# A perceiver-style kernel on one Trainium2 core: the context keys of the first cross attention transposed in 32x32 blocks on VectorE and put in place by copies

## The chip, the core and the metric

The kernel runs on one core of one Trainium2 chip, as one program. The metric is the device time of that program in microseconds. Shown are the median of three runs and, apart from it, one profiled execution, from which all durations come. The engines are called by the names of the profile: PE (TensorE's matmuls) and PEld (its weight loads), DVE (VectorE), ACT (ScalarE), POOL (GpSimd) and SP (SyncE, which here only issues DMAs).

## What is computed

A sequence `x` of 32 batches of 64 tokens with 256 features passes six layers, each added to `x`: a cross attention to a context of 256 tokens per batch, a linear attention, a gated feed-forward layer, a second cross attention, a recurrent layer and a mixture of experts. All is float32. The change touches the first layer alone, and the loading of the second layer's weights. The first layer, cut to what matters:

```python
x_ = layer_norm(context, ln1_g, ln1_b)      # 32 x 256 x 256
l  = layer_norm(layernorm(x), ln2_g, ln2_b) # 32 x 64 x 256
q  = l @ Wq                                 # 16 heads of 64
k, v = split(concat([x_, l], axis=1) @ Wkv) # 320 keys
w  = softmax((q * 64**-0.25) @ (k * 64**-0.25).T)
out = (w @ v) @ Wo
x  = x + out
```

## The kernel before

**Stages.** The first stage (until about 850 us) is this cross attention, batch by batch. Then linear attention, feed-forward, second cross attention and recurrence run together, interleaved over groups of two token tiles, and at the end the experts.

**The first stage.** Keys and values are never formed. A head's query is multiplied with the key weights instead, which gives a 256-wide vector `qk` per query and head, and scores are `qk` against the normalised context itself. The steps, by function:

- `l0_context(t)` loads the context of two batches into `cx` (two buffers), normalises it in place (`norm`) and applies the affine part on POOL (`affine`, two operations on 128 x 1024).
- `l0_queries(g)` does the same for four batches of latents, transposes them on PE (`tr_lat`), forms `q` (PE groups `pq`, evicted by ACT or DVE with the factor 0.125) and then `qk`: eight groups `pqk` per four batches, one per pair of heads, two PSUM banks each, so sixteen evictions.
- `l0_keys(b, ...)` makes `cT`, the transposed context of a batch (2 x 128 features by 256 tokens) followed by the 64 transposed latents. The context's four 128x128 blocks are transposed on PE (`tr_c`, against the identity) and one copy brings the bank to `cT` (two buffers). The latents come by one POOL copy.
- `l0_scores(b, ...)` runs eight PE groups `sc`, 128 rows (two heads x 64 queries) by 320 keys. For each, DVE takes the negated maximum (`nmax`), ACT the exponential with its sum. For every four groups DVE takes the reciprocal of the sums, scales (128 x 1280) and transposes in 32x32 blocks into `bT`, which has one buffer. Then sixteen block copies of 32 x 640 bring `bT` into `pT`: four on POOL, four on ACT or DVE, eight as DMAs issued by SP.
- `l0_applied(b, ...)` multiplies the context with `pT` (PE groups `pu`, four banks per batch) into `uT`; `l0_projected(t, ...)` applies value and output weights (`po`, `pw`) and adds to `x`.

**What sets the order.** The Python code does not issue instructions as it runs. Every operation is recorded in a plan (`Plan`), with a `rank` (its due time in units of a batch), and `run` then issues all of them in one order: at each step the operation that can start first by the planner's own cost table, the lower rank at a tie. An operation made with `either` or `copy` may go to ACT or DVE, whichever starts it first. The hardware executes each engine's instructions strictly in the order issued, each waiting for its own semaphores. Hence all instructions in the profile bear the line of the one place that issues them (L375), and groups are told apart by tile names.

**Memory.** Tiles of the large stages lie at fixed places of one `arena` of 45056 floats per partition. `ar.put(phase, tag, size, *at)` declares the places of a tag. Areas of a later phase may overlap those of an earlier one; their tiles then wait until every tile of the earlier tag has been released. PSUM has eight banks, shared by all.

Of the kernel before, what the change touches and what calls it, by code (L numbers as in the profile page):

```python
# [8 lines left out]
F32 = mybir.dt.float32  # L9
I32 = mybir.dt.int32  # L10
AF = mybir.ActivationFunctionType
ALU = mybir.AluOpType
AX = mybir.AxisListType

P = 128
B, S, D = 32, 64, 256
S2 = 256
# [192 lines left out]
class Plan:  # L210
# [12 lines left out]
    def __init__(self, tc):  # L223
        self.tc, self.ops, self.slots, self.news = tc, [], {}, []
        self.rank, self.group, self.lane, self.last = 0.0, None, None, {}
        for engine, attr in self.ENGINES.items():
            setattr(self, attr, PlanEngine(self, engine))
# [71 lines left out]
    def run(self, ahead):  # L299
# [7 lines left out]
        while todo:  # L307
            best, short = None, None
            while rest[-1] not in waiting:
                rest.pop()  # L310
            for op in sorted(ready, key=lambda op: op.rank):
                if short is not None and op.rank > short.rank and "PE" in op.ways and op.news:
                    continue
                if op.rank > rest[-1].rank + ahead:
                    continue
                at = 0.0
                if op.news and not self.has_room(op):
                    if "PE" in op.ways and (short is None or op.rank < short.rank) and self.has_room(op, True):
                        short = op
                    continue  # L320
                for engine, (length, _) in op.ways.items():
                    at = free[engine]
                    for other in op.before:
                        at = max(at, other.end if other.on == engine and other.end == other.done else other.done + self.HOP)
                    for t_ in op.uses:
                        at = max(at, t_.free_at)
                    key = at, op.rank
                    if best is None or key < best[0]:
                        best = key, op, engine
            assert best is not None, "nothing can start"  # L330
            (at, _), op, engine = best
            length, calls = op.ways[engine]
            todo -= 1
            ready.remove(op)
            waiting.remove(op)
            op.on = engine
            op.end = op.done = free[engine] = at + length
            busy[engine] += length
            if "dma" in calls[0][0]:
                size = PlanEngine.size_of(calls[0])  # L340
                wire = max(wire, op.end) + size / 380e3
                op.done = max(wire, op.end + size / 220e3) + (2.4 if engine == "POOL" else 1.5)
            self.issue(op, engine, calls)
            for other in op.after:
                other.left -= 1
                if other.left == 0:
                    ready.append(other)
# [91 lines left out]
class PlanEngine:  # L439
# [34 lines left out]
    def length(engine, name, args, kw):  # L474
# [18 lines left out]
        if engine == "POOL":  # L493
            return 0.7 if n < 64 else 0.3 + 2.0e-3 * n
        return 0.18 if name == "transpose" else max(0.36, 1.67e-3 * n)
# [3 lines left out]
def kernel(ctx: ExitStack, tc: tile.TileContext, d: dict, out: bass.AP):  # L499
# [130 lines left out]
    with ExitStack() as sa:  # L630
# [15 lines left out]
        for n in range(4):  # L646
            ar.put(1, f"W{n}", 2048, 2048 * n)
        ar.put(1, "q", 2048, 8192)
        ar.put(1, "gb", 1024, 10240)
# [12 lines left out]
        for tag, size, *at in (  # L662
            ("f_wg", 1536, 0), ("s_w", 512, 1536), ("f_wu", 1536, 2048), ("s_wp", 256, 3584), ("m_wr", 16, 3840),
            ("x_wq", 512, 4096), ("x_wk", 512, 4608), ("x_wv", 512, 5120), ("x_wo", 512, 5632), ("f_wd", 1536, 6144),
# [13 lines left out]
            ("g_tmp", 128, 41472), ("g_tmp2", 128, 41600), ("g_h", 128, 41728),  # L678
            ("a_wq", 512, 42496), ("a_wkv", 1024, 43008), ("rows_a", 1024, 44032),
        ):  # L680
# [38 lines left out]
        for t in range(2):  # L719
            pl.sync.dma_start(out=x[t], in_=d["x"][t * P : (t + 1) * P, :])  # L720

        wk = ar.tile([P, KD, 1024], F32, tag="q", name="wk")
        load_w(wk, "l0x_wkv", slice(0, 1024))
# [50 lines left out]
        def l0_context(t):  # L774
# [12 lines left out]
            if t == 2:  # L787

                nxt["a_wq"] = ar.tile([P, KD, D], F32, tag="a_wq", name="a_wq")
                pl.sync.dma_start(out=nxt["a_wq"], in_=d["a_wq"].rearrange("(k p) n -> p k n", p=P))  # L790
# [11 lines left out]
        def l0_queries(g):  # L802
# [20 lines left out]

            q = ar.tile([P, 8, G * S], F32, tag="q", name=f"q{g}")
            for j2 in range(4):
                pl.rank = G * g - 3.0 + 0.5 * j2
                pq = bank([P, 2, G * S], f"pq{g}_{j2}")
                with pl.together(1.75):
                    for jj in range(2):
                        for kd in range(KD):  # L830
                            mm(
                                pq[:, jj],
                                wq[:, kd, (2 * j2 + jj) * P : (2 * j2 + jj + 1) * P],
                                lt[:, kd, :],
                                start=(kd == 0),
                                stop=(kd == KD - 1),
                            )
                o = q[:, 2 * j2 : 2 * j2 + 2, :]
                pl.either(("mul", (o, pq, 0.125), {}), ("tensor_scalar", (o, pq, 0.125, None, ALU.mult), {}))
            pl.rank = G * g - 0.9  # L840
            qk = [None] * 8
            for n in range(8):
                j = 2 * (n % 4) + n // 4
                qk[j] = ar.tile([P, KD, G, 2, S], F32, tag="qk", name=f"qk{g}_{j}")
                pqk = [bank([P, KD, G * S], f"pqk{g}_{j}_{i}") for i in range(2)]
                with pl.together(1.0):
                    for kd in range(KD):
                        for i in range(2):
                            h_ = slice(64 * i, 64 * i + 64)
                            mm(pqk[i][:, kd], wkT[h_, j, kd * P : (kd + 1) * P], q[h_, j, :], start=True, stop=True)  # L850
                for i in range(2):
                    pl.copy(qk[j][:, :, :, i, :], pqk[i].rearrange("p k (b s) -> p k b s", b=G))
            return la, ls, lt, qk

        def l0_keys(b, lt, cx):

            pl.rank, pl.lane = b - 1.2, "k"
            b2, b4 = b % 2, b % G
            cT = ar.tile([P, KD, SK], F32, tag="cT", name=f"cT{b}")
            pst = bank([P, KD, S2], f"tr_c{b}")  # L860
            with pl.together(T4):
                for kd in range(KD):
                    for i in range(2):
                        tr(pst[:, kd, i * P : (i + 1) * P], cx[:, 2 * b2 + i, kd * P : (kd + 1) * P], ident)
            pl.gpsimd.tensor_copy(cT[:, :, S2:SK], lt[:, :, b4 * S : (b4 + 1) * S])
            pl.copy(cT[:, :, 0:S2], pst)
            return cT

        def l0_scores(b, cT, qk):
# [6 lines left out]
            pl.lane = "s"  # L876
            B_ = 32
            bT = ar.tile([P, 5, 4, 4, B_], F32, tag="bT", name=f"bT{b}")
            for jj in range(2):
                pr = ar.tile([P, 4, SK], F32, tag="pr", name=f"pr{b}_{jj}")  # L880
                sm = sp.tile([P, 4], F32, tag="sm", name=f"sm{b}_{jj}")
                for jp in range(4):
                    j = 2 * jp + jj
                    pl.rank = b - 1.6 + 0.1 * (4 * jj + jp)
                    sc = bank([P, SK], f"sc{b}_{j}")
                    with pl.together(1.1):
                        for kd in range(KD):
                            mm(
                                sc,
                                qk[j][:, kd, b % G].rearrange("p i s -> p (i s)"),  # L890
                                cT[:, kd, :],
                                start=(kd == 0),
# [8 lines left out]
                for n in range(2):  # L901
                    pl.vector.transpose(
                        bT[:, 2 * n + jj].rearrange("p k j c -> p j k c"),
                        pr[:, :, n * P : (n + 1) * P].rearrange("p j (k c) -> p j k c", c=B_),
                    )
# [5 lines left out]
            for n in range(4):  # L911
                for a in range(4):
# [4 lines left out]
                    )  # L917
                    if n == 0:
                        pl.gpsimd.tensor_copy(o, i_)
                    elif n < 2:  # L920
                        pl.copy(o, i_)
                    else:
                        pl.sync.dma_start(out=o, in_=i_)
            return pT
# [26 lines left out]
        def l0_projected(t, uT):  # L951
            pl.rank, pl.lane = 2 * t + 1.6, "p"
            oT = ar.tile([P, 8, P], F32, tag="oT", name=f"oT{t}", bufs=1)
            for j4 in range(2):
                po = bank([P, 4, P], f"po{t}_{j4}")
                with pl.together(1.87):
                    for jj in range(4):

                        j = 4 * j4 + jj
                        at = 4 * (j % 2) + j // 2  # L960
                        for kd in range(KD):
                            for i in range(2):
                                mm(
                                    po[64 * i : 64 * i + 64, jj, :],
                                    wv[:, kd, j * P + 64 * i : j * P + 64 * i + 64],
                                    uT[:, kd, at, i].rearrange("p b s -> p (b s)"),
                                    start=(kd == 0),
# [966 lines left out]
```

## Time and profile before

| | |
|---|---|
| median of three runs | 1628.32 us (1628.05 to 1630.23) |
| profiled execution, time | 1633.02 us |
| profiled execution, span from first to last instruction | 1631.3 us |
| mean granted TensorE clock | 0.991 |
| busy: PE, PEld, DVE, ACT, POOL | 97%, 68%, 67%, 43%, 26% |
| moved by DMA | 95.02 MB, mean 58 GB/s |

The page of the profile also divides the span into 40 slices; each digit is the busy share in tenths (9 is 90% or more), `PEclk` the granted clock:

```
PE   8999999999999999999989999999999999999996
PEld 6556656565665656666556777777776777878885
DVE  6657666676766757776755788888888788762230
ACT  4434344353533535334421454454544547432332
POOL 5123123230333223331311221221212112223342
PEclk9999999999999999999999999999999999999998
```

The first stage is slices 1 to 21. Busy time of PE is modelled, since matmuls are pipelined. In the profile a float32 matmul appears as two records (`sc`: 512 matmuls, 1024 records), a transpose as one (`tr_c`: 128). Groups of instructions are written `out<-in`, with the shape as partitions x elements, the count, the busy time and the mean of one, and after a bar the engine's idle time just before them with what ended it. In the timeline the columns are start, duration, engine, and the merged instructions; in square brackets stands how long the engine had been idle and who released it.

### The profile page before, as it was taken

To read this page: it belongs to the slowest core of one execution; us is meant where nothing else is said; L and a number is where in the kernel's file an instruction comes from. 1 tells how busy PE (TensorE), PEld (TensorE's weight loads), DVE (VectorE), ACT (ScalarE), POOL (GpSimd) and SP (SyncE) were. 2 spreads that over 40 slices of the span, in tenths; PEclk is the share of its full clock that TensorE was granted. 3 is DMA by queue.
4 is the path that set the end of the run, shared out by engine and by line. 5 is a ranking of instruction groups with operands and counts; after the bars stand their busy time and mean duration, and the time that the engine had idled before them with its cause. 6 is when DMAs were issued, how large, how long until landed. Compare 5 with 4: busy or idle time off the path is not lost. (4 is left out here: it accounts for less than half of the span.)

```text
span 1631.3 us, 25951 instructions
## 1 busy us (share of the span) xinstructions
PE 1579.4 (97%) x9226; PEld 1106.8 (68%) x9226; DVE 1088.2 (67%) x3089; ACT 693.8 (43%) x1813; POOL 422.1 (26%) x524
## 2 busy tenths in 40 slices
PE   8999999999999999999989999999999999999996
PEld 6556656565665656666556777777777776878885
DVE  6657666676766757776755788888888788762230
ACT  4434344353533535334421454454544547432332
POOL 5123123230333223331311221221212112223342
PEclk9999999999999999999999999999999999999998
DMA  6112112121112211122121000010000220455391
GB/s 212 38 30 59 38 31 44 38 59 29 39 30 46 47 34 40 30 71 53 38 54 49 14 27 27 18 37 14 27 27 20 85 80 19 133 144 141 69 307 31
DMA packets 95601, 95.02 MB, mean 58 GB/s; under 512 B 9327, under 2 KB 85936, under 8 KB 95472
## 3 DMA queue, kind: packets, MB, share of 16 engines
q1 hardware_dynamic: 89952, 85.41, 19.2%
q0 software_dynamic: 5520, 7.94, 2.4%
q8 instruction: 74, 1.21, 0.3%
q14 instruction: 55, 0.45, 0.1%
HBM read 63.63 MB, written 7.47 MB: 44 GB/s over the span
## 5 line engine op out<-in xcount | busy, mean ns | idle before, releaser
L375 PE MATMUL pu<-arena 128*128 128x512 f32 (+1 forms) x768 | 301.0, 615 | 3.5 <-ACT arena L375 2.8
L375 PE MATMUL sc<-arena 128*128 128x320 f32 x1024 | 290.5, 436 | 0.0
L375 PEld LDWEIGHTS sc<-arena 128*128 128x128 f32 x1024 | 190.8, 190 | 95.3 <-issue 19.2
L375 ACT ACTIVATE arena<-sc,nmax 128x320 f32<-128x320 f32 x256 | 134.4, 527 | 250.3 <-DVE nmax L375 241.8
L375 PEld LDWEIGHTS pu<-arena 128*128 128x128 f32 (+1 forms) x768 | 113.9, 189 | 175.9 <-issue 159.1
L375 POOL COPY arena<-arena 32x640 f32<-32x640 f32 (+1 forms) x161 | 108.9, 676 | 404.1 <-DVE arena L375 300.4
L375 DVE TENSOR_REDUCE nmax<-sc 128x1 f32<-128x320 f32 x256 | 121.8, 484 | 105.5 <-PE sc L375 104.1
L375 POOL TENSOR_TENSOR arena<-arena 128x1024 f32<-128x1024 f32 (+3 forms) x72 | 118.5, 1646 | 166.6 <-DVE arena L375 109.7
L375 ACT ACTIVATE arena<-arena,xnm 128x256 f32<-128x256 f32 x256 | 127.1, 500 | 52.1 <-DVE xnm L375 51.9
L375 DVE COPY arena<-pu 128x512 f32<-128x512 f32 x62 | 42.7, 689 | 115.4 <-PE pu L375 115.2
L375 DVE CUSTOM_DVE_ANT_0 arena<-xsc,arena 128x256 f32<-128x256 f32 x256 | 101.2, 421 | 17.7 <-ACT arena L375 10.3
L375 DVE TENSOR_TENSOR arena<-arena,sm 128x1280 f32<-128x1280 f32 x64 | 108.1, 1690 | 2.2
L375 DVE STREAM_TRANSPOSE arena<-arena 128x512 f32<-128x512 f32 (+1 forms) x192 | 104.4, 594 | 3.6
L375 ACT COPY arena<-pu 128x512 f32<-128x512 f32 x66 | 38.4, 585 | 128.0 <-PE pu L375 128.0
L375 POOL DMA_INDIRECT out<-arena x25 | 39.6, 1585 | 102.8 <-DVE arena L375 71.2
L375 PE MATMUL pqk<-arena 64*128 64x256 f32 x512 | 63.1, 383 | 1.6 <-ACT arena L375 1.6
L375 PE MATMUL xpTp<-ident,arena 128*128 128x128 f32 x512 | 63.6, 274 | 0.9 <-ACT arena L375 0.9
L375 PE MATMUL xak<-arena 128*128 128x512 f32 x128 | 62.3, 610 | 0.0
L375 PEld LDWEIGHTS xpTp<-ident,arena 128*128 128x128 f32 x512 | 56.9, 141 | 7.2 <-DVE arena L375 2.2
L375 PE MATMUL xav<-arena 128*128 128x256 f32 x256 | 61.5, 384 | 0.0
L375 PEld LDWEIGHTS po<-arena 128*64 128x64 f32 x1024 | 55.5, 137 | 8.8 <-issue 8.3
L375 PE MATMUL mepha<-arena 128*128 128x256 f32 x256 | 60.1, 385 | 1.4 <-ACT arena L375 1.4
(395 smaller groups left out, 2800.9 us busy)
## 6 DMA issues: line engine op xcount, KB each, us to landing
arena<-in_m_w SPq DMA_DIRECT2D x26, 1024.0 KB
arena<-arena SPq DMA_DIRECT2D x256, 80.0 KB
arena<-in_ctx SPq DMA_DIRECT2D x32, 256.0 KB
arena<-in_ctxT SPq DMA_DIRECT2D x16, 512.0 KB
x<-in_x SPq DMA_DIRECT2D x16, 128.0 KB
arena<-in_l0x_wkv SPq DMA_DIRECT2D x2, 1024.0 KB
arena<-arena SPq DMA_DIRECT2D x16, 128.0 KB
out<-x SPq DMA_DIRECT2D x16, 128.0 KB
```

The costliest lines, as they stand in the source:

```text
L375: r = getattr(real, name)(*[get(a) for a in args], **{k: get(a) for k, a in kw.items()})
```

## The change

Four things are changed.

1. **Keys.** For every batch but the first, `l0_keys` no longer uses PE. DVE transposes the context in 32x32 blocks into a new tile `bC` (two buffers): two instructions of 128 x 512. Sixteen copies of 32 x 128 then bring the blocks to their partitions in `cT`: four on POOL, twelve on ACT or DVE (`move` with `min(n, 1)`, so never as DMAs). The rank of the keys goes from `b - 1.2` to `b - 2.6`. `cT` has a new layout, `[P, 5, KD, S]`, in which a score's 320 keys stand in another order; the transposes of the probabilities undo it. The POOL copy of the latents becomes contiguous.
2. **Queries.** `q` is four tiles with a buffer each instead of one; `wk`, which had shared `q`'s place, gets one of its own in phase 0. Heads are taken in plain order 0 to 7 in `qk`, scores and projection, instead of even pairs before odd ones.
3. **Late loads.** The loads of `a_wq`, `a_wkv`, `rows_a` and `rows` (some 1.7 MB), recorded with the third pair of batches, get rank 29.5 and move in SP's queue from the start to between batches 20 and 28. `a_wq` and `a_wkv` take over the place that `q` had; `xTa` and `qT` of the second stage move to the place of `bC`, `q` and one free place.
4. **Planner.** Its cost for a POOL copy goes from `0.3 + 2.0e-3 n` to `0.2 + 0.9e-3 n` us. A field `lean` is added to the choice between ACT and DVE; it stays 0.

The core of the diff:

```diff
-            return 0.7 if n < 64 else 0.3 + 2.0e-3 * n
+            return 0.7 if n < 64 else 0.2 + 0.9e-3 * n if name == "tensor_copy" else 0.3 + 2.0e-3 * n
...
-        ar.put(1, "q", 2048, 8192)
+        ar.put(0, "wk", 2048, 25856)
+        ar.put(1, "q", 512, 8192, 8704, 9216, 9728)
+        ar.put(1, "bC", 512, 42496, 43008)
...
-            ("xTa", 512, 8192, 8704), ("qT", 512, 9216, 9728), ("xn0a", 256, 10240), ("xn1a", 256, 10496),
+            ("xTa", 512, 42496, 43008), ("qT", 512, 9728, 43520), ("xn0a", 256, 10240), ("xn1a", 256, 10496),
...
-            ("a_wq", 512, 42496), ("a_wkv", 1024, 43008), ("rows_a", 1024, 44032),
+            ("a_wq", 512, 8192), ("a_wkv", 1024, 8704), ("rows_a", 1024, 44032),
...
             if t == 2:
 
+                pl.rank = 29.5
                 nxt["a_wq"] = ar.tile([P, KD, D], F32, tag="a_wq", name="a_wq")
...
+        def move(n, o, i):
+            if n == 0:
+                pl.gpsimd.tensor_copy(o, i)
+            elif n == 1:
+                pl.copy(o, i)
+            else:
+                pl.sync.dma_start(out=o, in_=i)
...
         def l0_keys(b, lt, cx):
             pl.rank, pl.lane = b - 1.2, "k"
             b2, b4 = b % 2, b % G
-            cT = ar.tile([P, KD, SK], F32, tag="cT", name=f"cT{b}")
-            pst = bank([P, KD, S2], f"tr_c{b}")
-            with pl.together(T4):
+            pl.rank = b - 2.6
+            cT = ar.tile([P, 5, KD, S], F32, tag="cT", name=f"cT{b}")
+            pl.gpsimd.tensor_copy(cT[:, 4], lt[:, :, b4 * S : (b4 + 1) * S])
+            if b == 0:
...
+                return cT
+            bC = ar.tile([P, 4, KD, 2, B_], F32, tag="bC", name=f"bC{b}")
+            for i in range(2):
+                pl.vector.transpose(
+                    bC[:, :, :, i].rearrange("p k d c -> p d k c"),
+                    cx[:, 2 * b2 + i].rearrange("p (d k c) -> p d k c", d=KD, c=B_),
+                )
+            for n in range(4):
+                for a in range(4):
+                    k = (a + n) % 4
+                    move(
+                        min(n, 1),
+                        cT[B_ * k : B_ * k + B_, a].rearrange("p d c -> p (d c)"),
+                        bC[B_ * a : B_ * a + B_, k].rearrange("p d i c -> p (d i c)"),
+                    )
             return cT
...
-                    j = 2 * jp + jj
+                    j = 4 * jj + jp
...
-                        pr[:, :, n * P : (n + 1) * P].rearrange("p j (k c) -> p j k c", c=B_),
+                        pr[:, :, 0:S2].rearrange("p j (k i c) -> p i j k c", i=2, c=B_)[:, n],
```

As built, the changed kernel has 4 `tr_c` matmuls instead of 128, 62 more DVE transposes, and 496 copies of 32 x 128: 160 on DVE, 212 on ACT, 124 on POOL. From the first group of the second stage's keys and values (`lakv`) on, PE's instructions stand in the old order.

More of the change, by code (lines that the diff above doesn't have):

```diff
@@ L224, in __init__ @@
         self.tc, self.ops, self.slots, self.news = tc, [], {}, []
-        self.rank, self.group, self.lane, self.last = 0.0, None, None, {}
+        self.rank, self.group, self.lane, self.last, self.lean = 0.0, None, None, {}, 0.0
         for engine, attr in self.ENGINES.items():
@@ L326, in run @@
                         at = max(at, t_.free_at)
-                    key = at, op.rank
+                    key = at + (self.lean if engine == "DVE" and len(op.ways) > 1 else 0.0), op.rank
                     if best is None or key < best[0]:
@@ L720 @@
             pl.sync.dma_start(out=x[t], in_=d["x"][t * P : (t + 1) * P, :])
-        wk = ar.tile([P, KD, 1024], F32, tag="q", name="wk")
+        wk = ar.tile([P, KD, 1024], F32, tag="wk", name="wk")
         load_w(wk, "l0x_wkv", slice(0, 1024))
@@ L822, in l0_queries @@
             pl.copy(lt, pst)
[L824 to L829, printed above, removed]
-                        for kd in range(KD):
[L831 to L852, printed above, removed]
@@ L853, in l0_queries @@
-            return la, ls, lt, qk
+            q, qk = [None] * 4, [None] * 8
+            for step in range(5):
+                if step < 4:
+                    pl.rank = G * g - 3.0 + 0.5 * step
+                    q[step] = ar.tile([P, 2, G * S], F32, tag="q", name=f"q{g}_{step}")
+                    pq = bank([P, 2, G * S], f"pq{g}_{step}")
+                    with pl.together(1.75):
+                        for jj in range(2):
+                            for kd in range(KD):
+                                mm(
+                                    pq[:, jj],
+                                    wq[:, kd, (2 * step + jj) * P : (2 * step + jj + 1) * P],
+                                    lt[:, kd, :],
+                                    start=(kd == 0),
+                                    stop=(kd == KD - 1),
+                                )
+                    o = q[step]
+                    pl.either(("mul", (o, pq, 0.125), {}), ("tensor_scalar", (o, pq, 0.125, None, ALU.mult), {}))
+                pl.rank = G * g - 0.9
+                for j in range(8) if step == 4 else ():
+                    qk[j] = ar.tile([P, KD, G, 2, S], F32, tag="qk", name=f"qk{g}_{j}")
+                    pqk = [bank([P, KD, G * S], f"pqk{g}_{j}_{i}") for i in range(2)]
+                    with pl.together(1.0):
+                        for kd in range(KD):
+                            for i in range(2):
+                                h_ = slice(64 * i, 64 * i + 64)
+                                mm(
+                                    pqk[i][:, kd],
+                                    wkT[h_, j, kd * P : (kd + 1) * P],
+                                    q[j // 2][h_, j % 2, :],
+                                    start=True,
+                                    stop=True,
+                                )
+                    for i in range(2):
+                        pl.copy(qk[j][:, :, :, i, :], pqk[i].rearrange("p k (b s) -> p k b s", b=G))
@@ L855, in l0_keys @@
+            return la, ls, lt, qk
+        B_ = 32
+        def move(n, o, i):
[5 more added lines that the diff above has]
+                pl.sync.dma_start(out=o, in_=i)
         def l0_keys(b, lt, cx):
@@ L858, in l0_keys @@
             b2, b4 = b % 2, b % G
-            cT = ar.tile([P, KD, SK], F32, tag="cT", name=f"cT{b}")
-            pst = bank([P, KD, S2], f"tr_c{b}")
-            with pl.together(T4):
-                for kd in range(KD):
[L863 to L866, printed above, removed]
+            pl.rank = b - 2.6
+            cT = ar.tile([P, 5, KD, S], F32, tag="cT", name=f"cT{b}")
+            pl.gpsimd.tensor_copy(cT[:, 4], lt[:, :, b4 * S : (b4 + 1) * S])
+            if b == 0:
+                pl.rank = b - 1.2
+                pst = bank([P, KD, S2], f"tr_c{b}")
+                with pl.together(T4):
+                    for kd in range(KD):
+                        for i in range(2):
+                            tr(pst[:, kd, i * P : (i + 1) * P], cx[:, 2 * b2 + i, kd * P : (kd + 1) * P], ident)
+                for kd in range(KD):
+                    pl.copy(
+                        cT[:, 0:4, kd, :].rearrange("p a (i c) -> p a i c", i=2),
+                        pst[:, kd, :].rearrange("p (i a c) -> p a i c", i=2, a=4),
+                    )
+                return cT
+            bC = ar.tile([P, 4, KD, 2, B_], F32, tag="bC", name=f"bC{b}")
+            for i in range(2):
+                pl.vector.transpose(
+                    bC[:, :, :, i].rearrange("p k d c -> p d k c"),
+                    cx[:, 2 * b2 + i].rearrange("p (d k c) -> p d k c", d=KD, c=B_),
+                )
+            for n in range(4):
[5 more added lines that the diff above has]
+                        bC[B_ * a : B_ * a + B_, k].rearrange("p d i c -> p (d i c)"),
+                    )
             return cT
@@ L876, in l0_scores @@
             pl.lane = "s"
-            B_ = 32
             bT = ar.tile([P, 5, 4, 4, B_], F32, tag="bT", name=f"bT{b}")
@@ L890, in l0_scores @@
                                 qk[j][:, kd, b % G].rearrange("p i s -> p (i s)"),
-                                cT[:, kd, :],
+                                cT[:, :, kd, :],
                                 start=(kd == 0),
@@ L917, in l0_scores @@
                     )
[L918 to L923, printed above, removed]
+                    move(n, o, i_)
             return pT
@@ L959, in l0_projected @@
                         j = 4 * j4 + jj
-                        at = 4 * (j % 2) + j // 2
                         for kd in range(KD):
@@ L965, in l0_projected @@
                                     wv[:, kd, j * P + 64 * i : j * P + 64 * i + 64],
-                                    uT[:, kd, at, i].rearrange("p b s -> p (b s)"),
+                                    uT[:, kd, j, i].rearrange("p b s -> p (b s)"),
                                     start=(kd == 0),
```

## The prediction, made before the changed kernel was run

> **What bounds the kernel now.** I read the page's busy rows first, then a table of windows, then TensorE's waits, then the transposes' own rows, and last the timeline at the two places where TensorE waits at all. The windows (busy time of PE, PEld, DVE, ACT, POOL, with counts, then granted clock and DMA) cover the start, two steady stretches of four batches each, and the end of the first stage:
>
> ```profile
> 0.00:100.00 100.00, 88.76 (x405) 59.11 (x406) 66.11 (x154) 43.51 (x103) 37.25 (x54) 0.98 0.39 114
> 420.00:524.00 104.00, 103.77 (x501) 65.50 (x500) 70.55 (x138) 44.23 (x107) 29.10 (x30) 1.00 0.19 39
> 524.00:628.00 104.00, 103.77 (x502) 65.54 (x501) 70.84 (x138) 44.23 (x107) 29.32 (x30) 1.00 0.18 39
> 800.00:900.00 100.00, 94.13 (x465) 59.20 (x464) 59.05 (x153) 23.41 (x56) 16.68 (x33) 0.97 0.21 50
> ```
>
> TensorE works 103.77 of 104 us; VectorE 68%, ScalarE 43%, GpSimd 28%. A busy PE row alone proves little, so here are TensorE's waits between 100 and 780 us (total, times, longest):
>
> ```profile
> PE pqk L375 <- ACT arena L375: 1.6, 7, 0.2
> PE pu L375 <- DVE arena L375: 0.6, 3, 0.2
> ```
>
> 2.2 us in 680: the stage runs at the pace of TensorE's queue, and work taken from that queue is worth its own time, as long as no other engine then ends a wait last. These two rows name where that would happen: the evictions of `pqk` by ScalarE, and `pu`, which needs the transposed probabilities `pT`.
>
> **Removed: 31 of 32 context transposes.** Four `tr_c` matmuls per batch; only batch 0 keeps them. In the timeline at 429 us, first a `pqk` place:
>
> ```profile
> 429.15 0.60 PE L375 MATMUL tr_c<-ident,arena 128*128 128x128 f32 x4
> 429.36 0.49 DVE L375 TENSOR_REDUCE nmax<-sc 128x1 f32<-128x320 f32 x1 [0.58 <-PE sc L375]
> 429.68 6.74 PE L375 MATMUL pqk<-arena 64*128 64x256 f32 x58
> ...
> 431.46 0.17 DVE L375 RECIPROCAL sm<-sm 128x4 f32<-128x4 f32 x1
> 431.66 1.49 DVE L375 TENSOR_TENSOR arena<-arena,sm 128x1280 f32<-128x1280 f32 x1
> 431.71 2.54 ACT L375 COPY arena<-pqk 128x512 f32<-128x512 f32 x5 [0.23 <-PE pqk L375]
> ...
> 434.52 1.47 ACT L375 COPY arena<-arena 32x640 f32<-32x640 f32 x2 [0.27 <-DVE arena L375]
> ...
> 436.02 2.06 ACT L375 COPY arena<-pqk 128x512 f32<-128x512 f32 x4
> ...
> 436.66 1.13 PE L375 MATMUL pqk<-arena 64*128 64x256 f32 x6 [0.23 <-ACT arena L375]
> ```
>
> The four start at 429.15 and the next work at 429.68: 0.53 us of TensorE's queue. At 485.33 two contexts stand together and `pq` follows at 486.21: 0.44 each. I take 0.49: 31 x 0.49 = **15.2 us**. [...]
>
> **Added.** Per batch: two VectorE transposes of 512 elements, 4 GpSimd copies and 12 copies on ScalarE or VectorE, all 32x128. The rows of 100 to 780 us that are nearest:
>
> ```profile
> L375 ACT COPY arena<-arena 32x640 f32<-32x640 f32 x52 | 37.6, 722 | 11.2 <-DVE arena L375 10.0
> L375 DVE COPY arena<-arena 32x640 f32<-32x640 f32 x52 | 43.4, 834 | 1.2
> L375 DVE STREAM_TRANSPOSE arena<-arena 128x512 f32<-128x512 f32 x104 | 67.9, 690 | 2.9
> L375 POOL COPY arena<-arena 128x128 f32<-128x128 f32 x26 | 8.8, 338 | 71.5 <-PE sc L375 71.1
> ```
>
> No 32x128 copy is in the trace on ACT or DVE. Bounds: not under 128/640 of the row (0.15, 0.17), not over the row. ACT's pairs take 1.47 us, 0.735 each; five PSUM copies of 512 take 2.54, about 0.96 ns an element; so 0.735 - 512 x 0.96 ns leaves 0.24 for 128 elements. For DVE, 1.04 ns an element leaves 0.834 - 0.53 = 0.30; I take 0.28. [...] As built, 212 of the 372 copies are on ScalarE, 160 on VectorE. Per four batches (104 us) VectorE gets 8 x 0.69 + 21 x 0.28 less one eviction = +10.8, to 81; ScalarE 27 x 0.24 less three evictions = +5, to 49; GpSimd 16 x 0.34 = +5.4, to 35. All fit under 102 us. Throughput costs nothing; what costs is **where these stand in the queues**.
>
> *Even batches.* Their VectorE transposes stand after two or so `nmax` and wait for GpSimd's affine of the new context (two of 2.57 us). Behind them on VectorE stand the next `nmax`. TensorE has four more score groups (4.3 us) and then `pu` (10.3 us) to do without a bank that only these `nmax` free; after the wait VectorE needs some 4 us. Cover is near 10 us: cost 0; uncovered, 1 us per us of wait.
>
> *Odd batches.* Buffer `cT` (two places) is free only when the last scores of batch b-2 are done, so their copies stand exactly between the last scores and the softmax chain: on VectorE one copy before the last `nmax` and four before the reciprocal, on ScalarE some three before the last exponential and four behind it.
> At the seven `pqk` places (one per query group after the first): today the first reciprocal comes 2.3 us after the scores' end (431.46 - 429.15), ScalarE being held by the `tr_c` eviction, and seven of 16 evictions are done before the `pT` copies. With the new order: `nmax` at 0.4 to 0.9, four copies to about 1.95, reciprocal 2.0; ScalarE exponential to 1.6, copies to 2.5, then only four evictions before its `pT` copies at about 5 (2.0 + 3.06, as 434.52 - 431.46 today), done 6.4, next eviction 7.0. Eight banks plus four evictions carry six of eight groups, to 5.7 to 6; the seventh waits for 7.0 and its second bank for 7.6. Stall about 1.5 against 0.4 today: 7 x 1.1 = **-7.7**.
> At the seven other odd places, scores of b+1 follow `pq` and then `pu`: today 0.88 + 3.46 + 7 x 1.08 = 11.9 us cover the `pT` chain, after it 3.46 + 8 x 1.08 = 12.1. The chain gets five copies in front, and loses the eviction that delayed the exponential: +0.4. Net 0.2 x 7 = **-1.4**.
>
> *Rest of the stage.* Where linear attention begins, `pT29` is covered by 0.44 + 1.73 + 7 x 1.08 = 9.7 us instead of 12.8 (a stall of 1.1 included), against a chain near 12: **-1.1**. The start: queries of group 1 come later, as their normalisation is queued behind the key copies, so eight score groups stand in a row before `pu0`: I work out 3 us of stall. Today's start has 2.8 us of the same kind at 76 to 79 us, with the clock at 0.87 behind it. Called equal, +-3. `q` in four pieces, plain order of heads, own place of `wk`: they change no count; TensorE waited 1.5 us for wk's own load and it still does. **Late loads** (a_wq, a_wkv, two rows, 1.7 MB): four SP issues past the middle of the stage; a_wq waits on `pqk` readers that end before the `pT` copies queued behind it are ready, and what it loads is used some two batches (50 us) later: 0. `xTa` now needs `bC` free, which it is a batch before. From `lakv0` on, TensorE's order is the old one, with its 5.3 us wait kept.
>
> Sum: 15.2 - 7.7 - 1.4 - 1.1 = **5.0 us gained**: the profiled execution's 1633.0 (span 1631.3) to 1628.0; against the median 1628.3, which lies 4.7 lower, **1623.3**.
>
> **Rivals.**
> *The whole gain stays* (-9 to -15, time about 1615): for it, 31% of VectorE idle and only 2.2 us of waits today; against it, eight banks cannot hold sixteen evictions. 0.20.
> [...]
> *Slower*: the short copies of odd batches stretch. Place: between last `nmax` and reciprocal, 14 times. Price: five copies each on the path. Break-even is 5.0/14 = 0.36 us per place, 0.07 a copy; at 0.42 us a copy instead of 0.28 it is 14 x 5 x 0.14 = 9.8, so 4.8 slower: 1633.1. For it: transposes already stretch from 0.594 to a mean of 0.690, and GpSimd copies keys at the same moment; against it: 0.834 was for 640 elements. 0.15.
> *It doesn't do what it says*: the planner may still leave transposes or lose all by order. The built order has 4 `tr_c` matmuls, so only 0.02.
>
> **Numbers.** Forecast 0.45, four fifths of it beyond 3.3 us. Faster 0.36 + 0.20 = 0.56; same 0.09 + 0.18 = 0.27; slower 0.17. The forecast's own range, start +-3 and stalls +-3, is 1619 to 1627; with the rivals until two in ten are out, 1614.0 to 1631.0.
>
> **What would show it.** In the after profile: `tr_c` x4; PE busy time of a steady stretch 102 us per four batches plus about 1.7 us of waits; `pqk` waiting for ACT in longer gaps; `pu` for DVE or DMA a little; 32x128 copies near 0.24 and 0.28; the `lakvs` stall unchanged. A stage with waits still near 2 us proves the whole gain; copies of 0.4 us or waits of TensorE on `sc` behind the VectorE transposes prove me wrong on the other side.

## The result: 0.3% slower, where a gain of 5 us was forecast

| | before | changed |
|---|---|---|
| median | 1628.21 us (20 runs, 1625.67 to 1635.18) | 1633.28 us (20 runs, 1629.27 to 1636.94) |
| ratio to before | | 1.0030, 95% interval 1.0020 to 1.0041 |
| profiled execution: span, mean granted clock | 1631.3 us, 0.991 | 1634.9 us, 0.987 |

The page of the changed kernel, its row of busy time:

```profile
PE 1575.4 (96%) x9102; PEld 1096.0 (67%) x9102; DVE 1135.6 (69%) x3300; ACT 743.1 (45%) x2006; POOL 449.8 (28%) x648
```

The transposes are gone from TensorE (9102 records, 124 fewer than the 9226 before), and the share of no engine has moved by more than two points. Nothing here looks like a bound that changed. TensorE's waits between 100 and 780 us (total, times, longest) show more:

```profile
PE pqk L375 <- ACT arena L375: 6.8, 7, 1.0
PE po L375 <- ACT arena L375: 1.5, 5, 0.3
PE tr_lat L375 <- POOL arena L375: 1.2, 1, 1.2
```

The seven `pqk` places now wait up to 1.0 us each, 0.2 before, and `po` waits, which it did not; the row of `pu` for VectorE is gone. The weight loads of the same `pqk` groups (PEld) waited longer than the matmuls. Their rows, first before and then changed:

```profile
PEld pqk L375 <- ACT arena L375: 5.6, 14, 0.6
PEld pqk L375 <- ACT arena L375: 15.1, 28, 1.4
```

The waits of the matmuls alone understate the loss. I lay the starts of TensorE's blocks in the two timelines beside each other, for one steady group of four batches (429.68 to 533.66 us before, 427.22 to 531.84 changed; a block lasts from its first matmul to the start of the next work):

| one group of four batches, us | before | changed | difference |
|---|---|---|---|
| `tr_c`, four contexts | 1.89 | 0 | -1.89 |
| `pqk`, 64 records | 8.03 | 9.70 | +1.67 |
| the `po` that now directly follows `pu` | 3.64 | 4.16 | +0.52 |
| all `sc` | | | +0.46 |
| `pw` | 7.02 | 6.91 | -0.11 |
| whole group | 103.98 | 104.62 | +0.64 |

So this group gives back all it gained and a third more (on the mean of six groups, below, 0.52 us are lost instead of 0.64). Of the 0.46 of `sc`, 0.16 fall on the scores between the second `pq` and `pu`, and the rest on other places. The `pqk` block measures 8.03 us at each of its seven steady places before, and 9.70 or 9.71 after: a difference this regular is no noise. The timeline of the changed kernel at such a place, to be read against the lines at 429 us in the prediction:

```profile
427.22 6.31 PE L375 MATMUL pqk<-arena 64*128 64x256 f32 x48
...
427.48 0.91 ACT L375 COPY arena<-arena 32x128 f32<-32x128 f32 x3
...
428.08 1.16 DVE L375 COPY arena<-arena 32x128 f32<-32x128 f32 x4
428.42 0.53 ACT L375 ACTIVATE arena<-sc,nmax 128x320 f32<-128x320 f32 x1
...
429.06 1.22 ACT L375 COPY arena<-arena 32x128 f32<-32x128 f32 x4
429.28 0.18 DVE L375 RECIPROCAL sm<-sm 128x4 f32<-128x4 f32 x1
...
430.30 2.05 ACT L375 COPY arena<-pqk 128x512 f32<-128x512 f32 x4
...
432.38 1.47 ACT L375 COPY arena<-arena 32x640 f32<-32x640 f32 x2
...
433.87 3.52 ACT L375 COPY arena<-pqk 128x512 f32<-128x512 f32 x7
...
434.51 2.48 PE L375 MATMUL pqk<-arena 64*128 64x256 f32 x16 [0.98 <-ACT arena L375]
```

This is the sequence of the prediction. Seven short copies on ScalarE and five on VectorE (one of them before these lines' row of four) stand before the first `pqk` eviction, which comes 3.08 us after the block's start. Four evictions are done before the `pT` copies (seven were), and the seventh of eight `pqk` groups waits for the next one: the 48 records ahead of the stop are six groups of two banks, which is the pool's eight banks and the four evicted.

The second loss is at the end of the stage, where linear attention begins with `tr_la` and `laq`:

```profile
794.63 0.60 PE L375 MATMUL tr_la<-ident,arena 128*128 128x128 f32 x4
...
795.19 0.91 ACT L375 COPY arena<-arena 32x128 f32<-32x128 f32 x3
...
796.77 1.22 ACT L375 COPY arena<-arena 32x128 f32<-32x128 f32 x4
...
798.06 0.58 ACT L375 COPY arena<-tr_la 128x512 f32<-128x512 f32 x1
...
798.70 3.78 PE L375 MATMUL laq<-arena 128*128 128x256 f32 x8 [3.47 <-ACT arena L375]
...
802.81 0.34 PEld L375 LDWEIGHTS sc<-arena 128*128 128x128 f32 x1 [0.20 <-issue]
...
803.34 0.34 PEld L375 LDWEIGHTS sc<-arena 128*128 128x128 f32 x1 [0.20 <-issue]
```

The eviction of `tr_la` stands behind seven key copies in ScalarE's queue (in this trace ScalarE's 1490 copies and activations start in just the order in which the plan issues them), and TensorE idles for 3.47 us (0.9 before). It could not have stood ahead of them. It writes `xTa`, which the change puts on the two places of `bC`, and these copies read the last `bC`. The program (`Area.room`) gives such a place away only when every `bC` tile has been taken and the one that lay there has been released. The last key copies end at 796.53 us on GpSimd, 796.84 on VectorE and 797.98 on ScalarE; the eviction starts at 798.06.

After the wait `laq`'s matmuls come every 0.43 us instead of every 0.22, and the first scores every 0.53 instead of every 0.27: the clock has dropped (granted clock 0.55 between 800 and 805 us). From `tr_la` to `lakvs` the changed kernel takes 55.58 us, the kernel before 50.53.

The ledger of the two profiled executions, as the lag of the changed one (minus: it is ahead): -2.85 us at the second `pqk` block, +0.25 at the eighth, +0.66 at `tr_la`, +5.71 at `lakvs`, +7.11 at the first feed-forward matmul, +3.6 at the end. What lies behind `lakvs` has TensorE's old order and varies by a few us from one profiled execution to the next, here +1.4 and then -3.5.

### The profile page after: what moved, and what is told of

Its sections match the earlier page's. It is cut to its first block, busy times and chain, and to the rows that moved or that the text cites. A ratio compares the mean times of both kernels' runs of the same rounds, so it can differ in the third digit from the quotient of the medians.

```text
span 1634.9 us, 26235 instructions
## 1 busy us (share of the span) xinstructions
PE 1575.4 (96%) x9102; PEld 1096.0 (67%) x9102; DVE 1135.6 (69%) x3300; ACT 743.1 (45%) x2006; POOL 449.8 (28%) x648
## 5 line engine op out<-in xcount | busy, mean ns | idle before, releaser
L375 POOL COPY arena<-arena 32x128 f32<-32x128 f32 (+2 forms) x285 | 144.4, 510 | 440.1 <-PE sc L375 228.3
L375 POOL TENSOR_TENSOR arena<-arena 128x1024 f32<-128x1024 f32 (+3 forms) x72 | 111.5, 1549 | 137.7 <-DVE arena L375 97.7
L375 ACT COPY arena<-arena 32x128 f32<-32x128 f32 (+1 forms) x276 | 108.9, 394 | 74.2 <-DVE arena L375 70.5
L375 DVE STREAM_TRANSPOSE arena<-arena 128x256 f32<-128x256 f32 (+1 forms) x254 | 128.5, 553 | 18.7 <-POOL arena L375 15.0
L375 DVE COPY arena<-arena 32x128 f32<-32x128 f32 (+2 forms) x225 | 96.2, 427 | 13.9 <-PE sc L375 9.8
L375 DVE TENSOR_TENSOR arena<-arena,sm 128x1280 f32<-128x1280 f32 x64 | 99.0, 1548 | 2.2
L375 ACT COPY arena<-pu 128x512 f32<-128x512 f32 x73 | 41.9, 585 | 127.9 <-PE pu L375 127.8
L375 DVE COPY arena<-pu 128x512 f32<-128x512 f32 x55 | 37.5, 682 | 68.0 <-PE pu L375 68.0
L375 PE MATMUL pqk<-arena 64*128 64x256 f32 x512 | 69.3, 391 | 6.8 <-ACT arena L375 6.8
L375 PEld LDWEIGHTS pqk<-arena 64*128 64x128 f32 x512 | 51.3, 186 | 24.8 <-ACT arena L375 15.1
```

The source lines that it names most:

```text
L375: r = getattr(real, name)(*[get(a) for a in args], **{k: get(a) for k, a in kw.items()})
```

## The experiments

My theory, T1: the key copies of the odd batches cost, through their place in the queues. With two `cT` buffers they can't start before the last scores, and so they stand ahead of the `pqk` evictions, and at the end ahead of `tr_la`'s eviction. (That this eviction also has to wait for `bC`, whatever the queue, was not part of T1.) The rivals were R1, the load of the added work as such, and R2, the late loads or another part of the change. Medians of different sets of runs aren't compared, because the kernel before itself read 1628.6, 1629.2 and 1632.8 us in the three sets; its ratio within the set is. "Group" is a sixth of the time from the second to the eighth `pqk` block.

| kernel | median, us | ratio to before (95%) | group | `pqk` block | `tr_la` to `lakvs` |
|---|---|---|---|---|---|
| before | 1628.21 | | 104.05 | 8.03 | 50.53 |
| changed | 1633.28 | 1.0030 (1.0020 to 1.0041) | 104.57 | 9.70 | 55.58 |
| third `cT` | 1622.29 | 0.9958 (0.9945 to 0.9972) | 102.79 | 8.15 | 53.72 |
| all copies on GpSimd | 1630.21 | 1.0009 (1.0001 to 1.0017) | 102.32 | 7.16 | 63.26 |
| TensorE at `pqk` | 1632.10 | 1.0023 (1.0014 to 1.0032) | 103.30 | 8.03 | 54.13 |
| TensorE at the end | 1630.56 | 1.0009 (0.9999 to 1.0019) | 104.58 | 9.70 | 50.32 |
| GpSimd, TensorE at the end | 1614.48 | 0.9911 (0.9888 to 0.9934) | 101.96 | 7.16 | 50.32 |
| third `cT`, TensorE at the end | 1621.45 | 0.9955 (0.9939 to 0.9972) | 102.86 | 8.15 | 50.32 |
| all keys on TensorE | 1628.03 | 0.9999 (0.9986 to 1.0012) | 104.15 | 8.03 | 50.26 |
| before, late loads | 1629.38 | 1.0000 (0.9989 to 1.0012) | 103.94 | 8.03 | 50.53 |
| TensorE at `pqk`, not batch 1 | 1630.73 | 0.9982 (0.9972 to 0.9993) | 103.31 | 8.03 | 54.10 |
| GpSimd from the fifth batch, TensorE at the end | 1618.15 | 0.9911 (0.9888 to 0.9933) | 102.01 | 7.16 | 50.32 |

### A third buffer for the transposed keys

```diff
-        ar.put(1, "cT", 640, 16384, 17024)
+        ar.put(1, "cT", 640, 16384, 17024, 43520)
```

> A third buffer for the transposed keys (cT), nothing else; TensorE's order of work through the loop stays that of the changed kernel. Theory T1 (the 0.49 us per batch is given back because with two cT buffers the copies of the odd batches start only after the last scores, in ScalarE's and VectorE's queues ahead of the evictions that free the pqk banks, and at the end ahead of the eviction of the linear attention's transposes): the pqk block falls from 9.7 us to about 8.0 (7 times -1.7 = -12), the 3.5 us wait of laq goes (-5), so about 1616 us, 1612 to 1622. Rival R1 (it is the sheer load of 16 copies and two transposes per batch on VectorE and ScalarE, wherever they lie): the copies are as many, the time stays at 1631 to 1636. Rival R2 (the late weight loads or another part of the change): stays at 1631 to 1636.

Measured: 0.9958, 1622.3 us, 0.3 us outside what T1 expected and far below what R1 and R2 expected; the group falls by 1.78 us, the `pqk` block by 1.55. The copies are as many, on the same engines (15 of them went from ScalarE to VectorE); what changed is when they run. **R1 falls.** Its row of waits between 100 and 780 us:

```profile
PE pqk L375 <- ACT arena L375: 2.5, 7, 0.4
```

At the end T1 was half right, and `laq` still waited 2.4 us. The last batch's key copies now run a batch's place earlier, but six of them still end on ScalarE at 783.89 us, after `tr_la` (783.23), and then a `pu` eviction and an exponential stand before `tr_la`'s eviction (785.04).

### All key copies on GpSimd

```diff
-                        min(n, 1),
+                        0,
```

> All 16 key copies of a batch on GpSimd in place of four there and twelve spread over VectorE and ScalarE. T1: nothing stands ahead of the pqk evictions or of the evictions at the end, the gain appears as with a third buffer: 1614 to 1622 us. R1, in the form that GpSimd or the chain transposes - GpSimd copies - scores is what holds the scores up: twelve more copies of 0.3 us make each batch's keys 3.6 us later, scores wait on POOL, 1636 us or more. If both are half right (odd batches' scores start late because GpSimd needs 4.8 us after the last scores): 1625 to 1632.

Measured: 1.0009, with a `pqk` block of 7.16 us and no wait at it: 0.87 better than before. ScalarE and VectorE now do eight of the sixteen evictions before `pT`'s copies (seven before the change, four in the changed kernel); with the eight banks, no group waits for a bank. Between the second and the eighth block the loop gained 10.4 us. Then 11.1 us went in one wait, which neither theory had. The timeline at that place:

```profile
778.18 15.30 POOL L375 COPY arena<-arena 32x128 f32<-32x128 f32 x37 [3.96 <-DVE arena L375]
...
793.52 0.58 ACT L375 COPY arena<-tr_la 128x512 f32<-128x512 f32 x1 [5.04 <-POOL arena L375]
...
794.15 3.35 PE L375 MATMUL laq<-arena 128*128 128x256 f32 x7 [11.12 <-ACT arena L375]
```

This is the wait of `tr_la`'s eviction for `bC`, now without a queue in front of it: ScalarE stands idle for 5.04 us and is released when GpSimd's row of copies, which read `bC`, ends (778.18 + 15.30 = 793.48). Where the last two batches stay off GpSimd, below, `laq` waits 0.7 us. In the changed kernel the same wait is shorter, since three engines share the copies and end them 2.8 us after `tr_la`.

### TensorE transposes at the `pqk` places only

```diff
-            if b == 0:
+            if b == 0 or b % 4 == 1:
```

> The batches whose key copies lie ahead of the pqk evictions (every fourth, seven of them) get their keys by TensorE transposes as before; the other 24 stay on VectorE. T1: seven times 0.5 us of transposes back, seven times 1.7 us of stall gone: -8 us against the changed kernel, 1622 to 1628. R1 (sheer load, spread over all batches): a quarter of the added load goes, a quarter of what the change gave back: 1628 to 1633 and the pqk block keeps most of its 9.7 us. The end of the stage keeps its 3.5 us wait by both.

Measured: 1.0023, 1632.1 us, outside what T1 expected and inside R1's range, although the loop did what T1 said: the `pqk` block is back at 8.03, and a group costs 1.27 us less than the changed kernel's, 1.18 expected (0.49 back, 1.67 gone). The loss is at the start, where batch 1 fell under the edit as well: its `tr_c` is issued ahead of `tr_lat`, and this waits for GpSimd's affine:

```profile
38.84 0.60 PE L375 MATMUL tr_c<-ident,arena 128*128 128x128 f32 x4
...
44.47 1.11 PE L375 MATMUL tr_lat<-ident,arena 128*128 128x128 f32 x4 [5.03 <-POOL arena L375]
```

The second `pqk` block begins at 119.23 us, 5.07 later than in the changed kernel (single executions of one and the same start differ by up to 3.0 us there, as said below). So I ran it again without batch 1:

```diff
-            if b == 0:
+            if b == 0 or b % 4 == 1 < b:
```

> As the run with TensorE transposes at the pqk blocks, but batch 1 keeps its keys on VectorE, so that the start is that of the changed kernel. In the earlier run the loop gained 7.6 us on the changed kernel between the second and the eighth pqk block, as T1 had it, and 5 us went before the second, where batch 1's transposes stood ahead of a wait for GpSimd. If the start is the whole of that miss: 1625 to 1629. If TensorE transposes at the pqk blocks give nothing: 1631 or more.

Measured: 0.9982 (1630.7 in a set where the kernel before read 1632.8, so 2.1 us under it; 1625 to 1629 was expected against a kernel before at 1628 or 1629). The group is the same, 103.31, and the second `pqk` block begins at 112.89. From the changed kernel's ratio it is 0.0048 down, 7.8 us; 7 x 1.18 = 8.3 was to be expected. **The term of the `pqk` blocks stands by its removal too**, and its seven places carry far more than the quarter of the loss that an even load would give them.

### TensorE transposes for the last two batches only

```diff
-            if b == 0:
+            if b == 0 or b >= 30:
```

> Only the last two batches get their keys by TensorE transposes. T1: the wait of laq for ScalarE (3.5 us, and the lower clock that follows it) goes, two transposes of 0.5 us come back: 4 to 7 us under the changed kernel, 1626 to 1629.5. R1 and R2: within 1 us of the changed kernel's 1633, or the stall appears at another instruction of the same place.

Measured: 1.0009, which is 0.0021 or 3.4 us under the changed kernel's ratio, the two intervals just apart; less than the 4 to 7 expected, though in the profile the stretch from `tr_la` to `lakvs` falls by 5.3 us, to which two transposes in front of it must be added. `laq` waits 0.7 us. The edit takes the last copies out of the queue and also frees `bC` long before `tr_la` (the last key copy ends at 741.7 us); a run with `xTa` at a place of its own, which would part the two, was not made. The windows behind the place (busy time and records of TensorE, granted clock, share and rate of DMA), first of the changed kernel:

```profile
780.00:800.00 20.00, 16.53 (x52) 0.94 0.05 11
800.00:820.00 20.00, 20.00 (x58) 0.89 0.17 33
```

and then of this one:

```profile
780.00:800.00 20.00, 19.27 (x70) 1.00 0.07 14
800.00:820.00 20.00, 20.00 (x89) 1.00 0.29 54
```

Between 800 and 820 us TensorE is wholly busy in both, but at 0.89 of its clock in the one and all of it in the other; busy time alone hides that. (The counts differ also because other blocks fall into the window.) In the changed kernel the lower clock followed a wait of 3.47 us, but `laq`'s 2.4 us with the third buffer were enough as well (the first scores behind it came every 0.53 us, granted clock 0.91 between 780 and 800 us). In the profile the term is plain; in the ratios its size, some 3.4 us, is below what one profiled execution says.

### Both terms together

GpSimd for the copies from the third batch on, TensorE for the last two batches:

```diff
-            if b == 0:
+            if b == 0 or b >= 30:
...
-                        min(n, 1),
+                        0 if b > 1 else min(n, 1),
```

> Key copies of the batches from the third on by GpSimd alone, and the keys of the last two batches by TensorE transposes. In the run with all copies on GpSimd the loop was the fastest yet (10.4 us gained on the kernel before between the second and the eighth pqk block), and 11 us went in one wait of laq: the eviction of the linear attention's transposes writes the slots that the blocks bC used, which GpSimd still reads. If that is the whole loss, taking both away shows at the end too: 1613 to 1619 us, no wait of laq over 1 us. If the loss moves to another instruction of the end: 1622 or more.

Measured: **0.9911, 1614.5 us**, within the expectation; 14.8 us under the kernel before in its set. Its waits between 100 and 780 us have no row of `pqk`:

```profile
PE tr_lat L375 <- POOL arena L375: 1.7, 1, 1.7
PE po L375 <- ACT arena L375: 1.5, 5, 0.3
PE pq L375 <- DVE arena L375: 0.8, 1, 0.8
```

With the third `cT` in place of GpSimd (its edit and that of the last two batches):

> Third cT buffer, and the keys of the last two batches by TensorE transposes. T1 has three separate terms, and the terms for the pqk blocks and for the end should add: with the third buffer alone 1622.3, of which some 2 to 4 us were still lost at laq (2.4 us wait, then three score matmuls at 533 ns): 1617 to 1621. If the two share one cause: 1621 to 1624.

Measured: 0.9955, 1621.5 us, so the median lies in the range of one shared cause. In the profile the terms add at the place (53.72 to 50.32 us from `tr_la` to `lakvs`, with two transposes of 0.5 us in front of it to be taken off); that would be some 2.4 us or 0.0015, and the ratio shows 0.0003. With intervals of 0.0013 and more to either side the two can't be told apart. Whether the terms add stays open.

Last, GpSimd only from the fifth batch on (`0 if b > 3`), because the combination's second `pqk` block began 4.3 us later than the changed kernel's:

> As the run with the copies on GpSimd and the last two batches on TensorE, but GpSimd takes all copies only from the fifth batch on, so that the start is the changed kernel's. In the earlier run the second pqk block began 4.3 us later than in the changed kernel. If the order at the start alone did that: 1609 to 1613. If the start depends on the clock of each run rather than on this order: 1613 to 1617.

Measured: 0.9911 again. The block did begin 2.7 us earlier, at 115.74, but the ratio does not show it; its interval is 0.0045 wide, 7 us. The median, 1618.15, belongs to the set in which the kernel before read 1632.8, so the expectation in us can't be held against it. Which order is best at the start is not settled.

### The other parts of the change

All keys by TensorE, the rest of the change kept (`if True:` in place of `if b == 0:`; for the new layout of `cT` the eviction of a context is two copies of 128 x 256), and the kernel before with the late loads and the moved tiles alone (rank 29.5 and the places of `a_wq`, `a_wkv`, `xTa`, `qT`):

> Everything of the change but the keys: all keys by TensorE transposes, with the late loads, q in four tiles, the changed order of heads and the planner's changed price. T1: what the change loses hangs on the key copies, so this is the kernel before: 1625.5 to 1631. R2 or another part of the change costs: 1632 or more, with the pqk block at 8 us and the loss elsewhere.

> The kernel before with only the late loads of the linear attention's weights (and the tiles whose places that moves). T1: nothing waits for them, 1625.5 to 1631. R2: the loads, or the places in memory that they wait for, delay the start of linear attention by some 3 to 5 us: 1631 to 1634 and a longer wait of laq or lakvs.

Measured: 0.9999 and 1.0000, with intervals that end at 1.0012. **R2 falls**: late loads, `q` in four tiles, order of heads and planner's price together are worth nothing that can be measured, and the whole 0.3% comes with the keys. At the end of the stage it takes both, the `bC` of the keys and the moved `xTa`: each of these two runs has only the second, and `laq` waits 0.7 and 0.9 us in them. The `po` block is 3.64 us everywhere in the run with the keys on TensorE, so its 0.52 belongs to the keys as well.

## Why the prediction was wrong

Three steps of its sum failed, worth 4.0, 3.9 and 2.6 us in the profile: the `pqk` term was too small, the start of linear attention had a wait that was put at nothing, and a wait of `po` was not in the sum.

- **Bound.** Right: TensorE's queue sets the pace, and work taken out of it is worth its own time. Four contexts gave 1.89 us a group, forecast 1.96.
- **The `pqk` places: mis-sized.** The mechanism was right to the instruction (forecast: reciprocal 2.0 us after the scores, `pT` copies at about 5, TensorE going on at 7.0; measured 2.06, 5.16 and 7.29), the size was not: +1.67 a place instead of +1.1. The term compared "about 1.5 against 0.4 today". Without any stall the block takes 7.16 us, as the runs with GpSimd show, so the stall was 0.87 before and is 2.54 now. Of the 2.54, 0.94 go before TensorE stops (48 records in 6.31 us instead of 5.37), 0.98 in the stop, and 0.62 behind it (16 records in 2.41 us instead of 1.79). The rows of PE's waits that the prediction leans on show only the stop: 0.23 a place before, and 6.8 us in seven places now, of 7 x 2.54 = 17.8 lost. The rest is matmuls that come at the pace of the evictions and count as busy. The weight loads' row, 5.6 and 15.1 us, shows most of it, against 7 x 0.87 = 6.1 and 17.8.
- **The price of the short copies.** ScalarE's in rows of four took 1.22 us, 0.305 each, against my 0.24. (2.54 us over 5 x 512 elements is 0.99 ns an element and not 0.96, which would have left 0.23.) On the mean of the 175 between 100 and 780 us they took 0.295. Seven such copies put the first eviction 0.45 us later than forecast; how much of that reaches the end of the block no run tells. VectorE's 0.29 in such a row against 0.28 was right, and its mean of 137 copies was 0.267; the 1.04 ns an element behind the 0.28 are the step between two of its rows of before, `xpo` with 420 ns for 128 x 256 and `ffu` with 687 ns for 128 x 512.
- **The price of the transposes.** Those of the keys are 128 x 256, not 128 x 512 as the change is described above, and took 413 ns on VectorE, not 690. In the steady group VectorE's busy time grew by 5.4 us (70.53 to 75.91), not 10.8. That throughput costs nothing holds all the more.
- **Other odd places: a term left out.** Forecast 0.2 a place; the scores and `pu` there lost 0.16. But the order of TensorE changed: `po` now directly follows `pu` and waits for its eviction, 0.52 us at five places. **Not in the sum.** I had followed VectorE's and ScalarE's queues there and not TensorE's own.
- **The end of the stage: a wait put at nothing.** "-1.1" was worked out from the cover of `pT29`. Of the new place of `xTa` the prediction says that it "needs `bC` free, which it is a batch before". That step failed: the last key copies read `bC` until 797.98 us, 2.75 us after `tr_la` was done, and its eviction had to wait for them. The stretch from `tr_la` to `lakvs` lost 5.0 us: 2.5 more of idle time, and the rest at the lower clock. With the moved places but no `bC` at all (the kernel before with late loads) the stretch is as before, 50.53.
- **Start and late loads.** Called equal and 0; the start was equal within 0.5 us in the profile (2.85 gained, 2.36 of it removed transposes), the loads are 0 by experiment. So close a hit is luck: in the run with TensorE at the end, whose instructions are the same up to there, the second `pqk` block begins 3.0 us earlier, at 111.17.
- **The rivals.** The one with the right sign had the wrong mechanism: short copies did not stretch (0.29, not 0.42), and that its figure, 1633.1, lies 0.2 us from the measured median is luck. Its sign for a stretch, transposes going from 0.594 to 0.690 us, was a misreading: 0.594 is the mean of a row of two shapes, 0.690 for 128 x 512 and 0.403 for 128 x 256. The 0.18 that the chances give to "same" beside the forecast's 0.09 (within 0.2%, 3.3 us) rest on a dearer ScalarE copy, a price that no trace of before shows; in the changed kernel it was 0.295 us on the mean.

In the profile the missed terms are 7 x 0.57 = 4.0 (`pqk`), 5 x 0.52 = 2.6 (`po`) and 3.9 (end): 10.5 us, between the 10 by which the medians miss the forecast and the 12 by which the ledger does at the first feed-forward matmul. With 3 us of spread at the start the agreement is no closer than that.

## What to carry to other kernels

When work leaves the engine that sets the pace, look for what queues behind it where it lands: here 16 short copies a batch, far from filling any engine, turned 0.9% of removed work into a loss of 0.3%, mainly by standing in front of evictions. The same copies gained 0.4% with a third buffer, and 0.9% on GpSimd, which evicts nothing here, once the last two batches' keys were back on TensorE. For a pipelined engine measure a block from its first instruction to the next work, and find its length without any stall: the waits of the matmuls showed less than half of the loss, those of the weight loads most of it. When a tile moves to a place that another one uses, look up the last instruction that reads that place. Treat a seam between stages as a place of its own, with its own list of who stands behind whom and of whose memory is taken over.

## What the hardware showed that I had not expected

- Between 100 and 780 us GpSimd's 32 x 128 copies took a mean of 304 ns when it made four per batch and 381 ns when it made all sixteen, while it was still done in time for the scores. The copies as such did not slow down, the median is 287 ns in both. 29 of 422 took 1.4 to 1.6 us (1 of 104 with four per batch), and each of these ran for at least 1.28 us beside VectorE's scaling of the probabilities (128 x 1280).
- After `laq`'s waits of 3.47 and of 2.4 us the next scores ran at half the rate (one every 0.53 us instead of 0.27); after 0.7 us in the run with TensorE at the end they did not (granted clock 1.00 between 780 and 820 us). At the start similar idle times, 3.20 and 3.05 us before the second `tr_lat`, left a granted clock between 50 and 55 us of 0.52 in the changed kernel and 1.00 in the run with TensorE at the end: nearly the same gap doesn't always cost the same. This is a part of the spread of single executions.
